# 320 products an edge, selectors with four parts, and window sums turned by VectorE on their way out of PSUM

## The chip, the core and the metric

The kernel runs on one core of one Trainium2 chip. A core has five engines with a queue of instructions each: TensorE (PE, with its weight loads as PEld), VectorE (DVE), ScalarE (ACT), GpSimd (POOL) and SyncE (SP, here only for DMA). The metric is the device time of one execution in microseconds (us). A time is the median of several runs.

## The reference

One layer of a graph network in float32, 12500 nodes and 400000 edges, the edges sorted by target node. A node has 160 numbers: 64 scalars (y0) and 32 vectors of three components (y1). Cut to what matters:

```python
h = relu(layernorm(x))                      # 12500 x 160
y0, y1 = h[:, :64] @ W_l1_0, einsum(h1, W_l1_1)
w = silu(edge_attr_16 @ fc_W1) @ fc_W2      # 192 weights an edge: w_a 64, w_b 64, w_c 32, w_d 32
ys0, ys1 = y0[src], y1[src]
e0, e1 = edge_attr_4[:, :1], edge_attr_4[:, 1:]
mid_a = w_a * ys0 * e0                      # 64
mid_d = w_d * einsum('euc,ec->eu', ys1, e1) # 32, over sqrt(3)
mid_b = (w_b * ys0)[:, :, None] * e1[:, None, :]   # 64 x 3
mid_c = (w_c * e0)[:, :, None] * ys1               # 32 x 3
z0 = scatter_add(concat(mid_a, mid_d), dst)        # 96 a node
z1 = scatter_add(concat(mid_b, mid_c), dst)        # 96 x 3 a node
out = x + skip(h) + linear(z0, z1)                 # W_l2_0, W_l2_1
```

(Scale factors and the factor of each node are left out.)

## The kernel before

**Node phase (0 to about 120 us).** Layer norm, the maps to y0 and y1, and y written to DRAM (y_d, 160 numbers a row). It also loads and scales the weights; wo holds the weights of the linear step behind the sums, as three blocks of 128 rows.

**Edge phase.** The edges stand as 3125 tiles of 128 edges, one edge a partition. A *batch* is GT = 4 tiles; there are 782. Sums are made over *windows* of 32 target nodes: 24 tiles a window where nodes have many edges, then 12, 8, 6, 4 and 3, in order of the edges, 598 windows in all; four windows make a *group* of 128 nodes (150 groups). The order of the code is the order of the work on every engine; nothing is rearranged. For batch b the loop issues:

1. weigh(b + 2): two matmuls on PE (L606) give the 192 edge weights of four tiles in a PSUM buffer pw (two buffers). ACT multiplies w_a and w_c by e0, tile by tile (L524, four instructions), and copies e1 and the window-relative target into the same buffer (L525).
2. In the first three batches of a group, a step for the group before: turn (three transposes on PE, L656, and ACT's copy za, L658), linear (three matmuls, L665, ACT's copy os, L667, and a 0/1 matrix "place" by DVE, L669), add (two matmuls, L677). Behind the products of the third, accumulate adds to the output rows (DVE, L688).
3. select(b + 1) and products(b + 1), all on DVE. The selector (L618, L620) is a 128 x 128 matrix a tile: for each of 32 nodes of the window the 0/1 entry, and that times each of the three parts of e1. The products (L530 to L537) are 256 an edge: mid_a, w_c e0 y1, mid_d (with a product, a sum over components and a product), and w_b y0.
4. sums(b): per tile one matmul (L640), selector by products, 128 x 256, added up in a PSUM buffer pz (two buffers). Rows 96 to 127 of the result are the plain sums, rows 0 to 95 those times e1; of the 128 x 256 only the plain sums of the first 192 columns and the e1 sums of the last 64 are used. When a window ends, ACT copies them out of PSUM in four instructions (L646, L648) into zs, 32 rows a window. A matmul is recorded as two in the profile.
5. gather(b + 4): four indirect DMAs on POOL (L573), each fetching 128 rows of y_d. The first of them waits, by an added dependency, for the last matmul of sums(b).
6. Every fourth batch, hidden_pair: two matmuls with 512 columns (L586) and ACT's silu (L591), for the hidden layer of the edge weights.

Between these steps stand smaller ones for the skip term (L705 to L731), and for 16 batches whose rows come from the core's own maps in place of y_d.

Engines wait for each other in these ways that the change touches: DVE's selector waits for ACT's L525 (of its batch); PE's sums wait for DVE's products; ACT's copies wait for PE's sums, and stand in ACT's queue ahead of the scaling for a later batch; PE's transposes wait for ACT's copies of the group's last window and stand ahead of the sums of the next batch; POOL waits for sums.

A path for edges whose target lies outside the window (a loop behind the main one) is compiled and does not run on this input.

Of the kernel before, what the change touches and what calls it, by code (L numbers as in the profile page):

```python
# [10 lines left out]
F32 = mybir.dt.float32  # L11
# [7 lines left out]
P = 128  # L19
# [6 lines left out]
PC = 256  # L26
ZC = 384
# [23 lines left out]
def kernel(  # L51
# [85 lines left out]
    wo = const.tile([P, 3, D], F32, name="wo")  # L137
# [11 lines left out]
    wor = ip.tile([P, 3, D], F32, name="wor")  # L149
# [115 lines left out]
    def edge_weight_loads():  # L265
# [14 lines left out]
        load(wor[0:M0 + M1, 0, 0:M0], w_l2_0)  # L280
        for rows, k, c in ((slice(96, P), 0, 0), (slice(0, 32), 1, 1), (slice(32, 64), 1, 2)):
            load(wor[rows, k, o1(c)], w_l2_1[M0:, :])
        for rows, k, c in ((slice(64, P), 1, 0), (slice(0, 64), 2, 1), (slice(64, P), 2, 2)):
            load(wor[rows, k, o1(c)], w_l2_1[0:M0, :])
# [5 lines left out]
    def edge_weights():  # L290
# [3 lines left out]
        nc.vector.tensor_scalar(wo[M0:M0 + M1, 0, 0:M0], wo[M0:M0 + M1, 0, 0:M0], 1.0 / math.sqrt(3.0), None, ALU.mult)  # L294
# [226 lines left out]
    def scale(pw, ev, n):  # L521

        for k in range(n):
            nc.scalar.activation(pw[:, k, 0:96], pw[:, k, 0:96], AF.Copy, scale=ev[:, k, 0:1])  # L524
        nc.scalar.activation(pw[:, :n, NW:NW + 4], ev[:, :n, 1:5], AF.Copy)  # L525

    def multiply(pr, tmp, wt, yg, n):

        y1 = yg[:, :n, M0:].rearrange("p t (c u) -> p t c u", c=3)
        nc.vector.tensor_tensor(tmp[:, :n, 0:3, :], y1, wt[:, :n, NW:NW + 3].unsqueeze(3).to_broadcast([P, n, 3, M1]),  # L530
                                ALU.mult)
        nc.vector.tensor_reduce(tmp[:, :n, 3, :], tmp[:, :n, 0:3, :].rearrange("p t c u -> p t u c"), AX.X, ALU.add)  # L532
        nc.vector.tensor_mul(pr[:, :n, 192:PC], wt[:, :n, 96:160], yg[:, :n, 0:M0])  # L533
        nc.vector.tensor_mul(pr[:, :n, 0:M0], wt[:, :n, 0:M0], yg[:, :n, 0:M0])  # L534
        nc.vector.tensor_mul(pr[:, :n, 96:192].rearrange("p t (c u) -> p t c u", c=3),  # L535
                             wt[:, :n, M0:96].unsqueeze(2).to_broadcast([P, n, 3, M1]), y1)
        nc.vector.tensor_mul(pr[:, :n, M0:96], wt[:, :n, 160:NW], tmp[:, :n, 3, :])  # L537

    with (
        tc.tile_pool(name="selp", bufs=4) as selp,  # L540
        tc.tile_pool(name="prod", bufs=3) as prod,
        tc.tile_pool(name="tmp", bufs=1) as tmpp,
# [8 lines left out]
        hids, rows, wts, sels, z_ps, z_sb, zT, o_sb, prs, sums_ps, summed = ({} for _ in range(11))  # L551
# [62 lines left out]
        def select(b):  # L614

            n, wt = slots_of(b), wts[b]
            sel = sels[b] = selp.tile([P, GT, 4, WN], F32, name="sel")[:, :n, :, :]
            nc.vector.tensor_tensor(sel[:, :, 3, :], iota[:, 0:WN].unsqueeze(1).to_broadcast([P, n, WN]),  # L618
                                    wt[:, :n, NW + 3:NW + 4].to_broadcast([P, n, WN]), ALU.is_equal)
            nc.vector.tensor_tensor(sel[:, :, 0:3, :], sel[:, :, 3:4, :].to_broadcast([P, n, 3, WN]),  # L620
                                    wt[:, :n, NW:NW + 3].unsqueeze(3).to_broadcast([P, n, 3, WN]), ALU.mult)

        def products(b):
            wt, yg = wts.pop(b), rows.pop(b)
            pr = prod.tile([P, GT, PC], F32, name="pr")
            tmp = tmpp.tile([P, GT, 4, M1], F32, name="tmp")
            multiply(pr, tmp, wt, yg, slots_of(b))
            prs[b] = pr

        def sums(b):  # L630
# [3 lines left out]
            for k, t in enumerate(tiles_of(b)):  # L634
# [7 lines left out]
                if last:  # L642
                    if w == 0:
                        z_sb[g] = post.tile([P, ZC], F32, name="zs")
# [169 lines left out]
        for b in range(NB):  # L814
# [13 lines left out]
            if g and k < K:  # L828
                (turn, linear, add)[k](g - 1)
# [202 lines left out]
```

## Time and profile before

| | |
|---|---|
| median of three runs | 4765.01 us (4756.0 to 4784.77) |
| profiled execution | 4774.96 us |
| its span, first to last instruction | 4773.1 us |
| granted TensorE clock, mean | 0.868 |
| PE busy | 78% of the span |
| DVE, POOL busy | 62% each |
| ACT busy | 46% |
| first and last gather start | 115.4 and 4749.3 us |

The span is what the profile covers; 1.9 us of the execution lie around it. Busy shares are averages over the whole span, and an engine that is not busy may be the one that everything waits for: POOL counts as busy only while it works on a gather (0.95 us of the 1.25 us from one to the next), so that a POOL with nothing but gathers would show about 76%. A releaser named "remote" means that the profile has no instruction of this core to put the end of the wait down to.

### The profile page before, as it was taken

What the parts mean: (1) busy time and instruction counts of PE and PEld (TensorE: products, weight loads), DVE (VectorE), ACT (ScalarE), POOL (GpSimd) and SP (SyncE); (2) the same over time, 40 slices, a digit from 0 to 9 for tenths busy, and PEclk for the clock granted to TensorE, in tenths of its full rate; (3) what the DMA queues carried; (4) which work ended last, traced back from release to release, by engine and by line L of the source; (5) the groups of instructions that cost most, each with busy time, mean ns of one, the idle gap of its engine ahead of it and who ended that gap; (6) DMA issues with size and microseconds to landing.
All of it is one profiled execution on the core that took longest, in us unless ns stands there. A gap on an engine that the chain in (4) does not pass through costs nothing.

```text
span 4773.1 us, 53679 instructions
## 1 busy us (share of the span) xinstructions
PE 3720.7 (78%) x13928; PEld 2551.0 (53%) x13928; DVE 2953.5 (62%) x8027; ACT 2205.2 (46%) x7512; POOL 2962.3 (62%) x3145
## 2 busy tenths in 40 slices
PE   7777778787777777777777777778777887788877
PEld 6455555455555554555555555555555555555555
DVE  5666666666666666656566656656566666666655
ACT  5333334344444443444444444444444455555555
POOL 5666666666656666666666666656665666665655
PEclk8888888888988888888888888888888888988988
DMA  7222222222222222222222222222222222222224
GB/s 192 67 60 64 63 62 65 60 65 66 61 62 65 66 70 66 66 63 69 65 69 63 66 62 64 67 62 64 62 66 65 64 66 63 68 66 66 64 58 115
DMA packets 262414, 328.99 MB, mean 69 GB/s; under 512 B 82776, under 2 KB 212104, under 8 KB 262104
## 3 DMA queue, kind: packets, MB, share of 16 engines
q0 software_dynamic: 150128, 256.23, 21.8%
q1 hardware_dynamic: 111478, 69.00, 5.2%
q8 instruction: 113, 1.85, 0.2%
q14 instruction: 197, 1.61, 0.1%
q10 hardware_dynamic: 498, 0.30, 0.0%
HBM read 307.66 MB, written 17.61 MB: 68 GB/s over the span
## 4 chain that ended last, share of the span: by engine, by line
PE 56%; another core or an unknown queue 15%; ACT 12%; issue 8%; DVE 7%; POOL 0%; DMA 0%; DVEq 0%; SPq 0%; ACTq 0%
PE pz L640 23%; PE pw L606 17%; ACT pw L524 6%; PE px L586 6%; PE px L665 3%; ACT zs L648 2%; PE px L656 2%; PE px L677 2%; DVE tmp L532 1%; DVE tmp L530 1%; ACT zs L646 1%; DVE pr L535 1%; DVE pr L534 1%; ACT pw L525 1%
## 5 line engine op out<-in xcount | busy, mean ns | idle before, releaser
L573 POOL DMA_INDIRECT yg<-y_d,src_q x3061 | 2896.2, 946 | 1748.8 <-issue 787.3
L640 PE MATMUL pz<-pr,sel 128*128 128x256 f32 x6250 | 1682.1, 417 | 38.1 <-ACT zs L648 36.1
L606 PE MATMUL pw<-w,hT 128*128 128x384 f32 x3126 | 1314.2, 547 | 304.3 <-DVE pr L537 111.7
L524 ACT ACTIVATE pw<-pw,ev 128x96 f32<-128x96 f32 x3125 | 984.9, 315 | 1199.1 <-remote 303.9
L640 PEld LDWEIGHTS pz<-pr,sel 128*128 128x128 f32 x6250 | 1289.4, 214 | 279.0 <-ACT zs L648 46.4
L606 PEld LDWEIGHTS pw<-w,hT 128*128 128x128 f32 x3126 | 619.2, 208 | 822.5 <-issue 377.2
L618 DVE TENSOR_TENSOR sel<-iota,pw 128x128 f32<-128x128 f32 x782 | 221.5, 283 | 1255.8 <-ACT pw L525 680.1
L646 ACT ACTIVATE zs<-pz 32x192 f32<-32x192 f32 x598 | 193.4, 323 | 801.0 <-remote 345.2
L532 DVE TENSOR_REDUCE tmp<-tmp 128x128 f32<-128x384 f32 x782 | 463.6, 593 | 31.1 <-remote 3.6
L586 PE MATMUL px<-xe,w 32*128 32x512 f32 x782 | 334.2, 750 | 161.0 <-ACT za L658 102.8
L620 DVE TENSOR_TENSOR sel<-sel,pw 128x384 f32<-128x384 f32 x782 | 432.7, 553 | 39.8 <-remote 8.0
L530 DVE TENSOR_TENSOR tmp<-yg,pw 128x384 f32<-128x384 f32 x766 | 419.6, 548 | 55.4 <-DMA yg<-y_d,src_q 48.8
L535 DVE TENSOR_TENSOR pr<-pw,yg 128x384 f32<-128x384 f32 x766 | 419.2, 547 | 0.0
L648 ACT ACTIVATE zs<-pz 32x64 f32<-32x64 f32 x1794 | 383.1, 214 | 24.4
L656 PE MATMUL px<-ident,zs 128*128 128x128 f32 (+1 forms) x450 | 129.3, 362 | 301.3 <-ACT zs L646 259.2
L533 DVE TENSOR_TENSOR pr<-pw,yg 128x256 f32<-128x256 f32 x766 | 317.0, 414 | 0.0
L534 DVE TENSOR_TENSOR pr<-pw,yg 128x256 f32<-128x256 f32 x766 | 316.9, 414 | 0.0
L591 ACT ACTIVATE hT<-px 128x512 f32<-128x512 f32 x391 | 216.1, 594 | 212.2 <-PE px L586 86.7
L656 PEld LDWEIGHTS px<-ident,zs 128*128 128x128 f32 (+1 forms) x450 | 69.7, 159 | 411.9 <-ACT zs L646 307.7
L586 PEld LDWEIGHTS px<-xe,w 32*128 32x128 f32 x782 | 90.2, 218 | 282.3 <-ACT za L658 123.4
L665 PEld LDWEIGHTS px<-wo,za 128*128 128x128 f32 x900 | 163.6, 222 | 108.0 <-ACT hT L591 36.2
L537 DVE TENSOR_TENSOR pr<-pw,tmp 128x128 f32<-128x128 f32 x782 | 219.2, 280 | 0.0
(139 smaller groups left out, 2210.2 us busy)
## 6 DMA issues: line engine op xcount, KB each, us to landing
yg<-y_d,src_q POOLq DMA_INDIRECT x3061
xe<-in_e SPq DMA_DIRECT2D x784, 32.0 KB
xs<-in_x SPq DMA_DIRECT2D x48, 160.0 KB
acc<-in_x SPq DMA_DIRECT2D x11, 640.0 KB
y_d<-ys SPq DMA_DIRECT2D x11, 640.0 KB
out<-acc SPq DMA_DIRECT2D x11, 640.0 KB
raw<-in_e SPq DMA_DIRECT2D x32, 192.0 KB
src_q<-in_src SPq DMA_DIRECT2D x32, 48.0 KB
```

The source lines that it names most:

```text
L524: nc.scalar.activation(pw[:, k, 0:96], pw[:, k, 0:96], AF.Copy, scale=ev[:, k, 0:1])
L530: nc.vector.tensor_tensor(tmp[:, :n, 0:3, :], y1, wt[:, :n, NW:NW + 3].unsqueeze(3).to_broadcast([P, n, 3, M1]), ALU.mult)
L532: nc.vector.tensor_reduce(tmp[:, :n, 3, :], tmp[:, :n, 0:3, :].rearrange("p t c u -> p t u c"), AX.X, ALU.add)
L533: nc.vector.tensor_mul(pr[:, :n, 192:PC], wt[:, :n, 96:160], yg[:, :n, 0:M0])
L534: nc.vector.tensor_mul(pr[:, :n, 0:M0], wt[:, :n, 0:M0], yg[:, :n, 0:M0])
L535: nc.vector.tensor_mul(pr[:, :n, 96:192].rearrange("p t (c u) -> p t c u", c=3), wt[:, :n, M0:96].unsqueeze(2).to_broadcast([P, n, 3, M1]) ...
L573: fetch = nc.gpsimd.indirect_dma_start(out=yg[:, slot(t), :], out_offset=None, in_=y_d, in_offset=bass.IndirectOffsetOnAxis(ap=ev4[t // BL ...
L586: nc.tensor.matmul(ph, w1[r, :], xe[r, :], start=True, stop=True)
L606: nc.tensor.matmul(pw[:, 2 * k:2 * k + m, 0:NW], hT[:, o:o + P], w2[:, :m, :], start=True, stop=True)
L620: nc.vector.tensor_tensor(sel[:, :, 0:3, :], sel[:, :, 3:4, :].to_broadcast([P, n, 3, WN]), wt[:, :n, NW:NW + 3].unsqueeze(3).to_broadcast ...
L640: mm = nc.tensor.matmul(pz[:, 0:PC], sel[:, slot(t), :, :], pr[:, slot(t), :], start=o == 0, stop=last)
L648: nc.scalar.activation(zs[:, 192 + M0 * c:192 + M0 * (c + 1)], pz[WN * c:WN * (c + 1), 192:PC], AF.Copy)
```

## The change

It moves the four parts of e (e0 and the three of e1) out of the products and into the selectors. The selector's 128 columns are now the 0/1 entry times each of e0, e1x, e1y and e1z. The products of an edge are then free of e, and 320 in number: w_a y0, w_c y1 (96), w_b y0 and w_d y1 (96). ACT no longer scales; one instruction copies e's four parts and the relative target. On DVE the reduction over components goes, two products are one instruction and the others two of the same shape.

A window's sums are 128 x 320. Of them the first 32 rows (times e0) of the first 160 columns are used, and all rows of the last 160. VectorE takes them out of PSUM as transposes in squares of 32 by 32 (L639, L640 of the changed kernel), so that za, the operand of the linear step, is there without a turn on PE. za has five blocks of 128 rows in place of three, and some of them are zero weights; linear has five matmuls. The turn step goes, and linear and add stay at the second and third batch of the next group.

```diff
-PC = 256
-ZC = 384
+PC = 320
+ZC = 448
+ZK = 5
...
     def scale(pw, ev, n):
-        for k in range(n):
-            nc.scalar.activation(pw[:, k, 0:96], pw[:, k, 0:96], AF.Copy, scale=ev[:, k, 0:1])
-        nc.scalar.activation(pw[:, :n, NW:NW + 4], ev[:, :n, 1:5], AF.Copy)
+        nc.scalar.activation(pw[:, :n, NW:NW + 5], ev[:, :n, :], AF.Copy)
-    def multiply(pr, tmp, wt, yg, n):
+    def multiply(pr, wt, yg, n):
         y1 = yg[:, :n, M0:].rearrange("p t (c u) -> p t c u", c=3)
-        nc.vector.tensor_tensor(tmp[:, :n, 0:3, :], y1, wt[:, :n, NW:NW + 3].unsqueeze(3).to_broadcast([P, n, 3, M1]),
-                                ALU.mult)
-        nc.vector.tensor_reduce(tmp[:, :n, 3, :], tmp[:, :n, 0:3, :].rearrange("p t c u -> p t u c"), AX.X, ALU.add)
-        nc.vector.tensor_mul(pr[:, :n, 192:PC], wt[:, :n, 96:160], yg[:, :n, 0:M0])
-        nc.vector.tensor_mul(pr[:, :n, 0:M0], wt[:, :n, 0:M0], yg[:, :n, 0:M0])
-        nc.vector.tensor_mul(pr[:, :n, 96:192].rearrange("p t (c u) -> p t c u", c=3),
-                             wt[:, :n, M0:96].unsqueeze(2).to_broadcast([P, n, 3, M1]), y1)
-        nc.vector.tensor_mul(pr[:, :n, M0:96], wt[:, :n, 160:NW], tmp[:, :n, 3, :])
+        nc.vector.tensor_mul(pr[:, :n, :].rearrange("p t (x u) -> p t x u", x=2)[:, :, :, 0:M0],
+                             wt[:, :n, 0:NW].rearrange("p t (x u) -> p t x u", x=2)[:, :, :, 0:M0],
+                             yg[:, :n, 0:M0].unsqueeze(2).to_broadcast([P, n, 2, M0]))
+        for x in range(2):
+            nc.vector.tensor_mul(pr[:, :n, D * x + M0:D * (x + 1)].rearrange("p t (c u) -> p t c u", c=3),
+                                 wt[:, :n, 96 * x + M0:96 * (x + 1)].unsqueeze(2).to_broadcast([P, n, 3, M1]), y1)
...
-        def select(b):
...
         def products(b):
+            n, wt, yg = slots_of(b), wts.pop(b), rows.pop(b)
+            own = selp.tile([P, GT, WN], F32, name="own")
             sel = sels[b] = selp.tile([P, GT, 4, WN], F32, name="sel")[:, :n, :, :]
+            pr = prs[b] = prod.tile([P, GT, PC], F32, name="pr")
+            nc.vector.tensor_tensor(own[:, :n, :], iota[:, 0:WN].unsqueeze(1).to_broadcast([P, n, WN]),
+                                    wt[:, :n, NW + 4:NW + 5].to_broadcast([P, n, WN]), ALU.is_equal)
+            nc.vector.tensor_tensor(sel, own[:, :n, :].unsqueeze(2).to_broadcast([P, n, 4, WN]),
+                                    wt[:, :n, NW:NW + 4].unsqueeze(3).to_broadcast([P, n, 4, WN]), ALU.mult)
+            multiply(pr, wt, yg, n)
...
-                    nc.scalar.activation(zs[:, 0:192], pz[96:P, 0:192], AF.Copy)
-                    for c in range(3):
-                        nc.scalar.activation(zs[:, 192 + M0 * c:192 + M0 * (c + 1)],
-                                             pz[WN * c:WN * (c + 1), 192:PC], AF.Copy)
-        def turn(g):
...
+                        zT[g] = post.tile([P, ZK, P], F32, name="za")
+                    pz, at_w = z_ps.pop((g, w)), slice(WN * w, WN * (w + 1))
+                    nc.vector.transpose(zT[g][:, :, at_w], pz[:, D:PC].rearrange("p (k u) -> p k u", k=ZK))
+                    nc.vector.transpose(zT[g][0:32, :, at_w], pz[0:32, 0:D].rearrange("p (k u) -> p k u", k=ZK))
         def linear(g):
-            for k in range(3):
-                nc.tensor.matmul(po[:m, :], za[:, k, :m], wo[:, k, :], start=k == 0, stop=k == 2)
+            for k in range(ZK):
+                nc.tensor.matmul(po[:m, :], za[:, k, :m], wo[:, k, :], start=k == 0, stop=k == ZK - 1)
...
-            if g and k < K:
-                (turn, linear, add)[k](g - 1)
+            if g and 0 < k < K:
+                (linear, add)[k - 1](g - 1)
...
-                select(b + 1)
                 products(b + 1)
```

The loads and the scaling of wo follow its five blocks (more and smaller loads on SP in the node phase).

How the order of instructions moves, at three places. Rows of consecutive instructions of one engine; names are buffers, and x2 is two alike. First DVE, around the step linear of a group in the middle of the edges. Before:

```order
L618 TENSOR_TENSOR sel<-iota,pw 128x4x32
L620 TENSOR_TENSOR sel<-sel,pw 128x4x96
L530 TENSOR_TENSOR tmp<-yg,pw 128x4x96
L532 TENSOR_REDUCE tmp<-tmp 128x4x32
L533 TENSOR_TENSOR pr<-pw,yg 128x4x64
L534 TENSOR_TENSOR pr<-pw,yg 128x4x64
L535 TENSOR_TENSOR pr<-pw,yg 128x4x96
L537 TENSOR_TENSOR pr<-pw,tmp 128x4x32
L669 TENSOR_SCALAR place<-iota,at 128x256
```

The same place on DVE in the changed kernel:

```order
L617 TENSOR_TENSOR own<-iota,pw 128x128
L619 TENSOR_TENSOR sel<-own,pw 128x512
L530 TENSOR_TENSOR pr<-pw,yg 128x8x64
L534 TENSOR_TENSOR pr<-pw,yg 128x4x96 x2
L650 TENSOR_SCALAR place<-iota,at 128x256
L617 TENSOR_TENSOR own<-iota,pw 128x128
L619 TENSOR_TENSOR sel<-own,pw 128x512
L530 TENSOR_TENSOR pr<-pw,yg 128x8x64
L534 TENSOR_TENSOR pr<-pw,yg 128x4x96 x2
L639 STREAM_TRANSPOSE za<-pz 128x5x32
L640 STREAM_TRANSPOSE za<-pz 32x5x32
```

Eight instructions a batch are five, and at the end of a window two transposes have come in, which wait for the last matmul of that window's sums: behind the products of the batch after it, ahead of those of the next.

Second, ACT at such a place, where a window ends in nearly every batch. Before:

```order
L525 ACTIVATE pw<-ev 128x4x4
L658 ACTIVATE za<-px 128x384
L646 ACTIVATE zs<-pz 32x192
L648 ACTIVATE zs<-pz 32x64 x3
L591 ACTIVATE hT<-px 128x512 x2
L524 ACTIVATE pw<-pw,ev 128x96 x4
L525 ACTIVATE pw<-ev 128x4x4
L667 ACTIVATE os<-px 128x160
L646 ACTIVATE zs<-pz 32x192
L648 ACTIVATE zs<-pz 32x64 x3
```

ACT there in the changed kernel:

```order
L696 ACTIVATE sT<-px 128x512
L525 ACTIVATE pw<-ev 128x4x5
L588 ACTIVATE hT<-px 128x512 x2
L525 ACTIVATE pw<-ev 128x4x5
L648 ACTIVATE os<-px 128x160
```

The scalings, the copies of window sums and the turn's copy are gone; no instruction of ACT waits for sums any more.

Third, PE from the last sums of a group to the linear step of it. Before:

```order
L640 MATMUL pz<-pr,sel 128x256 x4
L606 MATMUL pw<-w_94,hT 128x2x192 x2
L656 MATMUL px<-ident,zs 128x128 x3
L640 MATMUL pz<-pr,sel 128x256 x4
L586 MATMUL px<-xe,w_93 128x512 x2
L606 MATMUL pw<-w_94,hT 128x2x192 x2
L665 MATMUL px<-wo,za 128x160 x3
```

And in the changed kernel:

```order
L633 MATMUL pz<-pr,sel 128x320 x4
L603 MATMUL pw<-w_94,hT 128x2x192 x2
L633 MATMUL pz<-pr,sel 128x320 x4
L583 MATMUL px<-xe,w_93 128x512 x2
L603 MATMUL pw<-w_94,hT 128x2x192 x2
L646 MATMUL px<-wo,za 128x160 x5
```

The three transposes between weigh and the next batch's sums are gone, the sums have 320 columns, and the linear step, at its old place, has five matmuls.

86 lines of the change are left out of this document (39 added, 47 removed).

## The prediction

> **What bounds the kernel now.** I read the busy totals and the chain first, then single gathers in the timeline, then the stages, then the waits.
>
> ```profile
> PE 3720.7 (78%) x13928; PEld 2551.0 (53%) x13928; DVE 2953.5 (62%) x8027; ACT 2205.2 (46%) x7512; POOL 2962.3 (62%) x3145
> PE 56%; another core or an unknown queue 15%; ACT 12%; issue 8%; DVE 7%; POOL 0%; DMA 0%; DVEq 0%; SPq 0%; ACTq 0%
> PE pz L640 23%; PE pw L606 17%; ACT pw L524 6%; PE px L586 6%; PE px L665 3%; ACT zs L648 2%; PE px L656 2%; PE px L677 2%; DVE tmp L532 1%; DVE tmp L530 1%; ACT zs L646 1%; DVE pr L535 1%; DVE pr L534 1%; ACT pw L525 1%
> ```
>
> No engine is full. PE is nearest with 78% and carries 56% of the chain, but 15% of the chain (716 us of 4773) is waiting that the trace can put on no engine. The stages say more (the last row is all gathers: shortest, median and longest in ns, first and last start):
>
> ```profile
> 120.00:1000.00 880.00, 671.31 (x2449) 458.97 (x2448) 556.28 (x1445) 341.67 (x1122) 550.93 (x582) 0.87 0.25 63
> 1000.00:2000.00 1000.00, 771.89 (x2853) 526.11 (x2852) 631.36 (x1661) 425.44 (x1424) 632.38 (x669) 0.87 0.26 65
> 3000.00:4000.00 1000.00, 792.89 (x2880) 535.44 (x2881) 606.16 (x1627) 496.04 (x1725) 614.52 (x650) 0.85 0.26 64
> L573 POOL DMA_INDIRECT yg<-y_d,src_q x3061: 940/946/1337, 115.4 to 4749.3; - x192
> ```
>
> Columns: the stretch, its length, then busy time and count of PE, PEld, DVE, ACT, POOL, and the granted clock. ACT's work grows from 0.39 to 0.50 of a stage, because windows close more often late in the edges; the number of gathers per 1000 us stays at 661, 669 and 650. So the pace does not follow ACT's load, and hardly the windows. On average a gather comes every (4749.3 − 115.4)/3060 = 1.514 us, and the gathers fill the span from 115.4 on: whatever the change does, it does it by letting gathers go sooner or later.
>
> ```profile
> 2519.85 0.95 POOL L573 DMA_INDIRECT yg<-y_d,src_q  x1 [0.30 <-issue]
> 2522.77 0.94 POOL L573 DMA_INDIRECT yg<-y_d,src_q  x1 [1.97 <-PE px L677]
> 2524.01 0.94 POOL L573 DMA_INDIRECT yg<-y_d,src_q  x1 [0.30 <-issue]
> ...
> 2536.51 0.95 POOL L573 DMA_INDIRECT yg<-y_d,src_q  x1 [0.30 <-issue]
> 2540.18 0.94 POOL L573 DMA_INDIRECT yg<-y_d,src_q  x1 [2.72 <-remote]
> ```
>
> Inside a run gathers start 1.25 us apart; between runs POOL stands still until the sums it waits for are known. Twelve gathers took 2540.18 − 2522.77 = 17.41 us, 1.45 each. What ends such a stop is odd (start, length, engine, line; the idle time before and its releaser in brackets; sums count two records a tile):
>
> ```profile
> 2530.30 1.89 PE L640 MATMUL pz<-pr,sel 128*128 128x256 f32 x8
> 2539.95 0.32 ACT L646 ACTIVATE zs<-pz 32x192 f32<-32x192 f32 x1 [5.94 <-remote]
> 2541.62 1.97 PE L665 MATMUL px<-wo,za 128*128 128x160 f32 x6 [4.33 <-ACT hT L591]
> ...
> 4756.73 0.32 ACT L646 ACTIVATE zs<-pz 32x192 f32<-32x192 f32 x1 [0.45 <-PE pz L640]
> ```
>
> The sums end at 2532.19, but ACT's first copy of them starts at 2539.95, after the run of gathers has ended and 5.94 us idle, put down to "remote": no instruction of the trace. After the last gather (4749.3) such a copy follows its sums after less than half a microsecond. I read it so: **while POOL issues gathers, PE's completion signals can reach ACT and POOL late, mostly when the run ends.** A long run then costs one hold per 8 or 12 gathers, a short one a hold per 4. Taking 1.457 us (11.66 us for 8, which fits the twelve above) for runs of 8 and more, the edges would end at 115.4 + 3060 × 1.457 = 4574, and with the 23.8 us behind the last gather the span would be 4598. The profiled span is 4773.1, so **about 175 us is lost above that floor**. This loss is what a change of waits can win, and what it can make larger.
>
> **The change part by part.** The sums are against the profiled run, 4774.96 us, which lies 10 us above the median of 4765.01.
>
> ```profile
> L640 PE MATMUL pz<-pr,sel 128*128 128x256 f32 x6250 | 1682.1, 417 | 38.1 <-ACT zs L648 36.1
> L665 PE MATMUL px<-wo,za 128*128 128x160 f32 x900 | 172.5, 334 | 46.7 <-ACT hT L591 28.3 <-ACT za L658 15.3 <-DVE acc L731 1.7
> L656 PE MATMUL px<-ident,zs 128*128 128x128 f32 (+1 forms) x450 | 129.3, 362 | 301.3 <-ACT zs L646 259.2
> L524 ACT ACTIVATE pw<-pw,ev 128x96 f32<-128x96 f32 x3125 | 984.9, 315 | 1199.1 <-remote 303.9
> L646 ACT ACTIVATE zs<-pz 32x192 f32<-32x192 f32 x598 | 193.4, 323 | 801.0 <-remote 345.2
> L648 ACT ACTIVATE zs<-pz 32x64 f32<-32x64 f32 x1794 | 383.1, 214 | 24.4
> L658 ACT ACTIVATE za<-px 128x384 f32<-128x384 f32 x150 | 73.0, 487 | 82.0 <-remote 65.7 <-PE px L586 8.0 <-PE pz L640 3.3
> L618 DVE TENSOR_TENSOR sel<-iota,pw 128x128 f32<-128x128 f32 x782 | 221.5, 283 | 1255.8 <-ACT pw L525 680.1
> L620 DVE TENSOR_TENSOR sel<-sel,pw 128x384 f32<-128x384 f32 x782 | 432.7, 553 | 39.8 <-remote 8.0
> L532 DVE TENSOR_REDUCE tmp<-tmp 128x128 f32<-128x384 f32 x782 | 463.6, 593 | 31.1 <-remote 3.6
> L533 DVE TENSOR_TENSOR pr<-pw,yg 128x256 f32<-128x256 f32 x766 | 317.0, 414 | 0.0
> L534 DVE TENSOR_TENSOR pr<-pw,yg 128x256 f32<-128x256 f32 x766 | 316.9, 414 | 0.0
> L537 DVE TENSOR_TENSOR pr<-pw,tmp 128x128 f32<-128x128 f32 x782 | 219.2, 280 | 0.0
> L736 DVE TENSOR_TENSOR oh<-iota,xp 128x512 f32<-128x512 f32 x16 | 11.0, 689 | 0.0
> L688 DVE SCALAR_TENSOR_TENSOR acc<-px,a_sb,acc 128x160 f32 x300 | 114.6, 382 | 149.4 <-PE px L677 71.8 <-PE pz L640 28.0 <-remote 21.5
> ```
>
> *PE.* A tile's sums (two records) took 1682.1/3125 = 0.538 us for 256 columns; 320 columns add a quarter, 0.135 × 3125 = **+421**. The linear step took 172.5/450 = 0.383 a matmul; two more for each of 150 groups, **+115**. The turn goes: **−129**. Together +406, 0.52 us a batch of 782, and PE's busy time becomes about 4127, 88% of a span of 4690. These durations are at the mean clock, 0.87 in the stages' rows. In one stretch of the stop above it was half:
>
> ```profile
> 2539.00:2540.00 1.00, 0.00 (x0) 0.00 (x0) 0.00 (x0) 0.05 (x1) 0.00 (x0) 0.50 0.00 0
> ```
>
> PE (first column) had stood idle and the granted clock (0.50) with it. [...]
>
> *ACT.* The four scalings of a batch go (−985), the four copies at a window's end (−193 − 383) and the turn's copy (−73): −1634, so about 571 is left. No work is added but a fifth value in L525. ACT stops being anyone's limit: between weigh's matmuls and DVE stand 0.2 us instead of four scalings and a copy, some 1.4 us less.
>
> *DVE, batch work.* The 512-element instructions are put at 689 (L736). Selector: 689 in place of 553. Two products of 256 elements become one of 512: 689 in place of 414 + 414. The reduction and the last product go (593 + 280); the product with e1 becomes a second one of L535's shape, with no difference. Sum −876 ns × 782 = **−685**. If the broadcast reads of the new 512-element ones run slower, by no more than a second pass over 128 elements (283) each, that is 443 less of the gain.
>
> *DVE, transposes.* 598 windows × 2, a kind of instruction the trace does not show. From below L618's 283 ns (128 elements, half of its input from PSUM) = 338; from above L532's 593, the only one that reads in another order than it stores = 709. I take 0.32, between L618 and L688's 382 for 160 elements from PSUM and nearer the first, since one of the two has only a quarter of the lanes: **+383**. DVE in sum −302 (between −347 and +24 for the transposes alone). [...]
>
> *What moves.* The copies out of PSUM leave ACT's queue, where they stood ahead of a later batch's scaling, and enter DVE's, between products(b+1) and products(b+2). So the late signal that stopped ACT now stops DVE. Behind the waiting transpose stand the selectors and products of b+2, then PE's sums for b+2 and, through the PSUM buffer that DVE frees, weigh's matmuls for b+4; behind the sums POOL's next gathers. PE itself loses a wait: L656 stood 301.3 us idle, 259.2 of it for ACT's copies, with sums of the next batch behind. The linear step moves to where the data has long been ready.
>
> ```profile
> DVE sel L618 <- ACT pw L525: 680.1, 208, 9.7
> DVE sel L618 <- ACT pw L524: 415.9, 164, 8.4
> POOL yg L573 <- remote: 337.3, 141, 3.9
> ```
>
> DVE already stands 1096 us waiting for ACT (total, times, longest), mostly because ACT is itself held. That wait goes over into the transposes' wait for PE; it does not vanish. DVE's own work is no limit: 2953 − 302 = 2651, 57%.
>
> *Loads at the start.* wor is loaded in more pieces, on SP, before 115.4; PE's 89% of the first 120 us is the cover, and I cost it at nothing. If uncovered it is a few microseconds.
>
> **The sum.** By the chain's shares of 4773: sums 23% = 1098, a quarter more, +274; linear 3% = 143, two thirds more, +95; the copies L646 and L648 were on it for 3% = 143 of their 576 busy, a quarter, and the transposes with the same share give +96. Gone: L524 6%, L646, L648, L656 together 5%, L532 1%, 12% = 573. Net −108. By the gathers: the round trip from gather to sums gets shorter by about 1.0 us of products (593 + 280 and 414 + 414 − 689, less what the selector and the extra order hide) and longer by 0.54 of sums, about half a microsecond better, and the turn no longer cuts runs short, but the holds remain. So I let half of the 175 come back: −87, **4688, said as 4690 us**. Both reckonings agree on the sign and roughly on the size; the chain's assumes that nothing else takes the freed place, so I stay above it.
>
> **The rivals.**
>
> *Slower: DVE waits for held sums while PE is nearly full.* In the stage from 3000 on PE worked 792.89/650 × 8 = 9.76 us for 8 gathers; with 2 × 0.52 it is 10.8, in a run that lasts 11.66 at its best. If each run then has one hold that stops DVE, and with it PE, for the mean of POOL's "remote" waits, 337.3/141 = 2.39, eight gathers take 13.2 us instead of 8 × 1.514 = 12.11, +1.08. In the second half, some 1800 gathers or 225 runs of 8, three runs in five so hit give +146; the first half, where windows close in fewer batches, keeps 40% of the 87. Together +111, about **4890**; with every run +243 − 35, 4983. It decides where a stop of DVE is longer than PE's slack of 0.9 us a run. For it: PE on 56% of the chain, and its half clock after stops. Against: DVE now has 0.9 us a batch more slack, and ACT's queue can't hold anything.
>
> *No effect.* The gathers' own 1.25 us and the holds set the pace, whoever is held: 650 to 669 gathers per 1000 us at quite different loads of ACT speak for it, and the loss stays 175: **4775**, within 1% of before (1% is about what a measurement of this kernel can tell from no change). The case that the change fails to shift work is part of it: PE's extra 406 may just fill its gaps.
>
> *Much faster.* If the holds come from ACT's many instructions and not from POOL's gathers, they go with them, and POOL runs at its own 1.25: 115.4 + 3825 + 23.8 = 3964, which PE's 4127 forbids; at 1.35 it gives **4270**.
>
> **How the numbers follow.** Forecast (4600 to 4717) 0.42; slower 0.38; no effect 0.14; much faster 0.06. Faster by over 1% is the first and last, 0.48; the sign is so open because PE is charged 406 us in any case, and the gain lies in waits. The range leaves out the much faster case and the worst of the slower one: from 4540 (1.438 a gather, 1% better than the run of twelve had) to 4930 (midway between 4890 and 4983). The forecast's own range is 4600 to 4717.
>
> **What would show it.** In the profile after: PE busy 4050 to 4150; ACT near 570; DVE near 2650; two transposes of about 0.3 us; gathers in runs of 8 or more at 1.46 a gather, and fewer runs of 4. The forecast is wrong if DVE's waits for PE's sums exceed the 1096 us that it waited for ACT, if PE's clock falls below 0.86, or if the gathers of the late stages fall below 640 per 1000 us; the no-effect case shows as gathers per 1000 us unchanged and PE's idle time smaller by just what it is charged.

## The result, and the profile after

The changed kernel takes 4709.57 us (median of 4 runs, 4703.56 to 4713.89) against 4770.42 for the kernel before in the same comparison: a ratio of 0.9872, with a 95% interval of 0.9838 to 0.9905. That is 1.3% faster; 4690 was forecast, and the range was 4540 to 4930. The profiled execution has a span of 4708.8 us, 64.3 less than before.

The page of the changed kernel, first busy time, then the chain by engine and by line:

```profile
PE 3891.7 (83%) x14078; PEld 2542.2 (54%) x14078; DVE 2736.7 (58%) x6877; ACT 581.6 (12%) x1845; POOL 2968.3 (63%) x3145
PE 66%; another core or an unknown queue 15%; issue 7%; DVE 7%; ACT 2%; ACTq 1%; POOL 0%; DMA 0%; DVEq 0%; SPq 0%; POOLq 0%
PE pz L633 31%; PE pw L603 19%; PE px L646 6%; PE px L583 3%; DVE pr L534 2%; PE px L658 2%; DVE pr L530 1%; ACT hT L588 1%; ACTq L525 1%; DVE za L640 1%; DVE za L639 1%; PE po L457 1%; PE px L704 1%; POOL yg L570 0%
```

ACT has gone from 46% to 12%. PE is busier by 171 us and DVE less busy by 217. The share of the chain that waits for nothing the trace shows is 15% as before. The groups (busy us, mean ns of one, idle time before and what ended it):

```profile
L570 POOL DMA_INDIRECT yg<-y_d,src_q x3061 | 2901.9, 948 | 1681.5 <-issue 795.2
L633 PE MATMUL pz<-pr,sel 128*128 128x320 f32 x6250 | 1950.3, 457 | 17.6 <-DVE za L640 15.2
L603 PE MATMUL pw<-w,hT 128*128 128x384 f32 x3126 | 1233.8, 519 | 208.7 <-DVE pr L534 135.6
L639 DVE STREAM_TRANSPOSE za<-pz 128x160 f32<-128x160 f32 x598 | 206.5, 345 | 1298.9 <-PE pz L633 551.3
L534 DVE TENSOR_TENSOR pr<-pw,yg 128x384 f32<-128x384 f32 x1532 | 773.5, 546 | 0.0
L530 DVE TENSOR_TENSOR pr<-pw,yg 128x512 f32<-128x512 f32 x766 | 523.2, 683 | 126.8 <-DMA yg<-y_d,src_q 118.3
L646 PE MATMUL px<-wo,za 128*128 128x160 f32 x1500 | 320.2, 376 | 294.4 <-ACT hT L588 198.2
L619 DVE TENSOR_TENSOR sel<-own,pw 128x512 f32<-128x512 f32 x782 | 536.9, 687 | 28.1 <-issue 1.2
L617 DVE TENSOR_TENSOR own<-iota,pw 128x128 f32<-128x128 f32 x782 | 200.0, 256 | 177.1 <-ACT pw L525 133.8
L640 DVE STREAM_TRANSPOSE za<-pz 32x160 f32<-32x160 f32 x598 | 202.1, 338 | 20.5
L669 DVE SCALAR_TENSOR_TENSOR acc<-px,a_sb,acc 128x160 f32 x300 | 113.9, 380 | 113.2 <-PE px L658 70.8
```

The first row answers for the whole change. GpSimd's idle time ahead of gathers fell from 1748.8 to 1681.5, by 67.3 us, and the span by 64.3: what the change won shows as less time in which the gathers stand still. Counted from their starts (over 1.4 us apart is a stop), there are 351 stops in place of 388, and each is as long as before (2.10 and 2.08 us beyond the 1.25): fewer stops, not shorter ones. DVE's idle time has moved as well: 1255.8 us ahead of the selector became 1298.9 ahead of the transpose, and 177.1 ahead of the selector.

By stages (length, then busy time and count of PE, PEld, DVE, ACT, POOL, granted clock):

```profile
120.00:1000.00 880.00, 726.11 (x2542) 459.89 (x2541) 482.68 (x1086) 118.17 (x368) 572.80 (x604) 0.91 0.24 65
1000.00:2000.00 1000.00, 819.98 (x2904) 527.66 (x2903) 562.78 (x1337) 120.22 (x385) 639.00 (x674) 0.92 0.24 66
3000.00:4000.00 1000.00, 826.94 (x2970) 543.32 (x2971) 602.26 (x1520) 103.95 (x340) 624.20 (x659) 0.91 0.24 65
```

In the first 880 us 604 gathers start in place of 582, in the later ones 674 and 659 in place of 669 and 650 (and 672 in place of 663 from 2000 to 3000, not shown). So half of the gain, 22 of the 45 gathers by which it is ahead at 4000 us, falls in the stage where windows are long and close seldom. The clock is 0.91 to 0.92 in place of 0.85 to 0.87.

The holds are still there. The timeline of the changed kernel at a window's end (rows of PE, POOL, ACT and DVE, others left out):

```profile
2119.97 1.01 DVE L534 TENSOR_TENSOR pr<-pw,yg 128x384 f32<-128x384 f32 x2
...
2124.24 2.32 PE L633 MATMUL pz<-pr,sel 128*128 128x320 f32 x8
...
2132.18 0.94 POOL L570 DMA_INDIRECT yg<-y_d,src_q  x1 [0.31 <-issue]
2135.28 0.30 ACT L648 ACTIVATE os<-px 128x160 f32<-128x160 f32 x1 [4.03 <-remote]
2135.34 0.35 DVE L639 STREAM_TRANSPOSE za<-pz 128x160 f32<-128x160 f32 x1 [9.73 <-remote]
2135.64 0.95 POOL L570 DMA_INDIRECT yg<-y_d,src_q  x1 [2.52 <-remote]
```

The batch's sums end at 2126.56, and those of the window that L639 reads at 2125.48, inside the same row. ACT, DVE and POOL, which wait for different results of PE, go on within 0.36 us of each other, 8.7 us after the batch's sums, when the run of gathers has ended. Taking for each of the 598 windows the time from the end of its own last matmul to the start of the first instruction that reads its sums (ACT's L646 before, DVE's L639 after), 162 windows were read over 4 us late before, and 121 after.

### The profile page after: what moved, and what is told of

Read it like the earlier page. It is cut to its first block, busy times and chain, and to the rows that moved or that the text cites. A ratio compares the mean times of both kernels' runs of the same rounds, so it can differ in the third digit from the quotient of the medians.

```text
span 4708.8 us, 46910 instructions
## 1 busy us (share of the span) xinstructions
PE 3891.7 (83%) x14078; PEld 2542.2 (54%) x14078; DVE 2736.7 (58%) x6877; ACT 581.6 (12%) x1845; POOL 2968.3 (63%) x3145
## 4 chain that ended last, share of the span: by engine, by line
PE 66%; another core or an unknown queue 15%; issue 7%; DVE 7%; ACT 2%; ACTq 1%; POOL 0%; DMA 0%; DVEq 0%; SPq 0%; POOLq 0%
PE pz L633 31%; PE pw L603 19%; PE px L646 6%; PE px L583 3%; DVE pr L534 2%; PE px L658 2%; DVE pr L530 1%; ACT hT L588 1%; ACTq L525 1%; DVE za L640 1%; DVE za L639 1%; PE po L457 1%; PE px L704 1%; POOL yg L570 0%
## 5 line engine op out<-in xcount | busy, mean ns | idle before, releaser
L570 POOL DMA_INDIRECT yg<-y_d,src_q x3061 | 2901.9, 948 | 1681.5 <-issue 795.2
L633 PE MATMUL pz<-pr,sel 128*128 128x320 f32 x6250 | 1950.3, 457 | 17.6 <-DVE za L640 15.2
L603 PE MATMUL pw<-w,hT 128*128 128x384 f32 x3126 | 1233.8, 519 | 208.7 <-DVE pr L534 135.6
L639 DVE STREAM_TRANSPOSE za<-pz 128x160 f32<-128x160 f32 x598 | 206.5, 345 | 1298.9 <-PE pz L633 551.3
L534 DVE TENSOR_TENSOR pr<-pw,yg 128x384 f32<-128x384 f32 x1532 | 773.5, 546 | 0.0
L530 DVE TENSOR_TENSOR pr<-pw,yg 128x512 f32<-128x512 f32 x766 | 523.2, 683 | 126.8 <-DMA yg<-y_d,src_q 118.3
L646 PE MATMUL px<-wo,za 128*128 128x160 f32 x1500 | 320.2, 376 | 294.4 <-ACT hT L588 198.2
L619 DVE TENSOR_TENSOR sel<-own,pw 128x512 f32<-128x512 f32 x782 | 536.9, 687 | 28.1 <-issue 1.2
L646 PEld LDWEIGHTS px<-wo,za 128*128 128x128 f32 x1500 | 290.2, 246 | 364.7 <-ACT hT L588 226.5
L525 ACT ACTIVATE pw<-ev 128x20 f32<-128x20 f32 x782 | 149.6, 191 | 2624.1 <-PE pw L603 970.4
L617 DVE TENSOR_TENSOR own<-iota,pw 128x128 f32<-128x128 f32 x782 | 200.0, 256 | 177.1 <-ACT pw L525 133.8
L640 DVE STREAM_TRANSPOSE za<-pz 32x160 f32<-32x160 f32 x598 | 202.1, 338 | 20.5
L669 DVE SCALAR_TENSOR_TENSOR acc<-px,a_sb,acc 128x160 f32 x300 | 113.9, 380 | 113.2 <-PE px L658 70.8
```

What stands on the lines that cost most here:

```text
L530: nc.vector.tensor_mul(pr[:, :n, :].rearrange("p t (x u) -> p t x u", x=2)[:, :, :, 0:M0], wt[:, :n, 0:NW].rearrange("p t (x u) -> p t x u ...
L534: nc.vector.tensor_mul(pr[:, :n, D * x + M0:D * (x + 1)].rearrange("p t (c u) -> p t c u", c=3), wt[:, :n, 96 * x + M0:96 * (x + 1)].unsqu ...
L570: fetch = nc.gpsimd.indirect_dma_start(out=yg[:, slot(t), :], out_offset=None, in_=y_d, in_offset=bass.IndirectOffsetOnAxis(ap=ev4[t // BL ...
L603: nc.tensor.matmul(pw[:, 2 * k:2 * k + m, 0:NW], hT[:, o:o + P], w2[:, :m, :], start=True, stop=True)
L619: nc.vector.tensor_tensor(sel, own[:, :n, :].unsqueeze(2).to_broadcast([P, n, 4, WN]), wt[:, :n, NW:NW + 4].unsqueeze(3).to_broadcast([P, ...
L633: mm = nc.tensor.matmul(pz[:, 0:PC], sel[:, slot(t), :, :], pr[:, slot(t), :], start=o == 0, stop=last)
```

## The experiments

The theory at this point: **H**, GpSimd's gathers set the pace, because PE's signals reach others late while they are issued; the change wins where it makes fewer things wait for such a signal. Against it: **E**, the engines' own loop sets the time (PE is 66% of the chain), and GpSimd follows.

Ratios below are to the kernel before, measured beside each; the changed kernel stands at 0.9872.

### Without gathers

```diff
-            for k, t in enumerate(tiles_of(b)):
-                fetch = nc.gpsimd.indirect_dma_start(
-                    out=yg[:, slot(t), :], out_offset=None, in_=y_d, in_offset=...)
-                if k == 0 and b - AHEAD in summed:
+            n, lo = slots_of(b), b % 24 * GT * P
+            fetch = nc.sync.dma_start(yg[:, :n, :], y_d[lo:lo + n * P, :].rearrange("(t p) u -> p t u", p=P))
+            if True:
+                if b - AHEAD in summed:
                     tc.add_manual_dep(fetch.ins, summed[b - AHEAD], ...)
```

The kernel before with this edit:

> The kernel before with its rows of y fetched by one plain load a batch from SyncE (the same 640 byte rows in number, from fixed places) in place of four indirect gathers on GpSimd; what is computed from them is therefore not the layer. Theory H (GpSimd's gathers and the completion signals that come late while they run set the time): without gathers no wait of several us ends at 'remote', PE idles little, its clock rises to 0.97 or more, and the time falls to what PE needs, 3720 x 0.87 = 3240 at full clock plus the two ends, 3350 to 3700 us. Theory E (the engines' own loop sets the time and GpSimd only follows): within 3% of 4770.

The changed kernel with it:

> The changed kernel with the same replacement of its gathers. Theory H: 3892 x 0.906 = 3526 of PE at full clock plus the ends, 3600 to 3900 us, and now slower than the kernel before with the same replacement, by about PE's added work at full clock, 200 to 350 us. Theory E: within 3% of 4710, and still faster than before.

Measured: 3298.41 us (ratio 0.6887, 0.6847 to 0.6927) and 3541.87 (0.7395, 0.7353 to 0.7438). **Without gathers the change makes the kernel 7.4% slower** (3541.87/3298.41), and PE is busy for 96% and 98% of the time. Both times lie below H's ranges, by 52 and 58 us; their difference of 243 is inside the 200 to 350. The page, first of the kernel before, then of the changed one:

```profile
PE 3165.6 (96%) x13928; PEld 2305.5 (70%) x13928; DVE 2915.4 (89%) x8027; ACT 2203.7 (67%) x7512; POOL 65.8 (2%) x84
PE 78%; DVE 15%; ACT 4%; issue 2%; DMA 0%; SPq 0%; DVEq 0%; ACTq 0%
```

```profile
PE 3475.3 (98%) x14078; PEld 2317.9 (66%) x14078; DVE 2712.3 (77%) x6877; ACT 592.2 (17%) x1845; POOL 66.4 (2%) x84
PE 90%; DVE 7%; issue 0%; ACT 0%; DVEq 0%; ACTq 0%
```

"Another core or an unknown queue" has left the chain, and of the 598 windows none is read over 4 us late in either. The clock is 0.990 and 0.996. Near full clock the sums tell their price in full:

```profile
L640 PE MATMUL pz<-pr,sel 128*128 128x256 f32 x6250 | 1485.4, 381 | 0.0
```

```profile
L633 PE MATMUL pz<-pr,sel 128*128 128x320 f32 x6250 | 1817.9, 434 | 0.6 <-DVE za L640 0.6
```

That is +332.5 us, more than the difference of 243 between the two times. E is out: with gathers neither kernel runs at its own loop's speed.

Whose signals are late can be read directly. The trace also holds moments at which an engine raised its completion signal (not all: with gathers about six in ten of DVE's and ACT's, eight in ten of PE's). In the changed kernel 2367 of DVE's 2380 and 1034 of ACT's 1036 come within 0.1 us of the end of an instruction that raises one; of PE's only 1022 of 2231 do, and 136 come over 4 us behind the nearest such end. Without gathers 2727 of PE's 2796 come within 0.1 us. In the timeline above, PE's four instructions that raise it and end between 2124.40 and 2127.85 are matched by four raises between 2135.26 and 2135.44, and DVE's transpose starts at 2135.34. So PE's signals are held back, and the engines that wait for them are not slow themselves: DVE is busy for 2736.7 us with gathers and for 2712.3 without.

### Gathers that nothing reads

The plain loads as above, and behind them the four gathers of the batch, with the same dependency, into a tile "un" (three buffers) that no instruction reads.

> The changed kernel with plain loads for the rows that are used, and beside them the same gathers on GpSimd, paced by the same sums, into buffers that nothing reads. Theory H, by the issuing itself: the signals come as late as ever, since GpSimd issues as many gathers; 4600 to 4800 us. If instead the products' wait for the gathered rows (their landing) sets the time: near the run without gathers, under 4000 us.

Measured: 4738.10 us, ratio 0.9893 (0.9836 to 0.995), the time of the changed kernel. The long waits of DVE and ACT by "remote" are back (total, times, longest; first this run, then the changed kernel):

```profile
DVE za L649 <- remote: 478.4, 95, 13.7
ACT hT L598 <- remote: 422.4, 90, 12.8
```

```profile
DVE za L639 <- remote: 435.7, 86, 9.7
ACT hT L588 <- remote: 648.9, 112, 12.7
```

So it is not the rows' arrival that the time hangs on. That GpSimd issues 3061 gathers, with nobody reading what they fetch, costs 1196 us (4738.10 − 3541.87). Two things are in this sum. At 1.25 us each, with the 117.4 us ahead of the first and the 22.3 behind the last, the gathers alone need 3965 us, some 425 more than the kernel without them. The other 771 of the profiled span of 4735.8 are time in which they stop, waiting for sums.

### PE's larger sums taken back

```diff
-                mm = nc.tensor.matmul(pz[:, 0:PC], sel[:, slot(t), :, :], pr[:, slot(t), :], ...)
+                mm = nc.tensor.matmul(pz[:, 0:256], sel[:, slot(t), :, :], pr[:, slot(t), 0:256], ...)
-                    nc.vector.transpose(zT[g][:, :, at_w], pz[:, D:PC]...)
+                    nc.vector.transpose(zT[g][:, :, at_w], pz[:, 96:256]...)
```

> The changed kernel with the sums' matmuls over 256 of the 320 product columns (64 columns left out, so the sums are not complete); all else, the transposes too, stays. It takes back PE's largest added term, 1950 x 0.2 = 390 us of busy time. If PE is what the time is made of (66% of the chain): -150 us or more, below 4560. Theory H: PE fills its idle time, and the time moves by less than 60 us, 4650 to 4710.

Measured: 4715.0 us, 5 above H's range; ratio 0.985 (0.9805 to 0.9894), not to be told from the changed kernel's 0.9872. The sums' group, and then the page, show where the 330 us go:

```profile
L633 PE MATMUL pz<-pr,sel 128*128 128x256 f32 x6250 | 1620.1, 405 | 28.9 <-DVE za L640 19.1 <-issue 6.8 <-DVE za L639 1.6
```

```profile
PE 3642.9 (78%) x14078; PEld 2577.7 (55%) x14078; DVE 2728.5 (58%) x6877; ACT 581.6 (12%) x1845; POOL 2962.4 (63%) x3145
L570 POOL DMA_INDIRECT yg<-y_d,src_q x3061 | 2896.2, 946 | 1672.8 <-issue 803.2
```

PE is 249 us less busy, its granted clock in this run is 0.885 in place of 0.906, and GpSimd's idle time is 8.7 us less. The 64 added columns are free here, though the chain gives the sums 31% of the time.

### Parts taken out one by one

The kernel before without ACT's scaling (the four L524 a batch are left out):

```diff
-        for k in range(n):
-            nc.scalar.activation(pw[:, k, 0:96], pw[:, k, 0:96], AF.Copy, scale=ev[:, k, 0:1])
```

> The kernel before without ACT's four scalings by e0 a batch (985 us of ACT; the factor e0 is left out). Theory W (the gain is what the shorter way from weigh to DVE wins, by letting GpSimd's next run start earlier): 4680 to 4740 us. Rival T (the gain comes from the turn that is gone from PE): no change, 4750 to 4790.

Measured: 4718.63 us, ratio 0.9876 (0.9845 to 0.9907), −51 us.

The kernel before without the turn:

```diff
-            for k in range(3):
-                nc.tensor.transpose(pt[:, k, :m], zs[:m, P * k:P * (k + 1)], ident[:m, :m])
-            za = post.tile([P, 3, P], F32, name="za")
-            nc.scalar.activation(za[:, :, :m], pt[:, :, :m], AF.Copy)
-            zT[g] = za
+            zT[g] = za_all
```

> The kernel before without the turn: the three transposes a group and ACT's copy of them are left out and the linear step reads a constant; ACT's copies out of PSUM stay. Theory W: 4730 to 4780, at most 1% better, since 22 of the waits on PE go that held sums. Rival T: 4660 to 4720.

Measured: 4687.85 us, ratio 0.9825 (0.9801 to 0.985), −82 us. Each theory was right on one part and wrong on the other: W on the scaling, T on the turn. Both parts count. 129 us of PE and 73 us of ACT bring 82 us, and 985 us of ACT bring 51.

The changed kernel without the transposes (za is a constant), and with each transpose made twice:

```diff
-                    nc.vector.transpose(zT[g][:, :, at_w], pz[:, D:PC]...)
-                    nc.vector.transpose(zT[g][0:32, :, at_w], pz[0:32, 0:D]...)
```

> The changed kernel without the transposes: the linear step reads a constant, and DVE waits no more for sums. 409 us of DVE's work and its wait of 1300 us for sums go. If the new wait of DVE costs what the slower rival feared: 4620 or less, 2% under 4710. If the holds pass to whoever waits next: 4680 to 4720.

> The changed kernel with each transpose made twice (409 us more on DVE, nothing left out). If DVE's work lies on the path in each window: +200 us or more, 4900. If it fills idle time behind the holds: under 1% more, 4700 to 4755.

Measured: without them 4642.25 us, ratio 0.9731 (0.9708 to 0.9753), so the transposes with their wait cost 1.4%, some 67 us, a result between the two forecasts. With twice as many the kernel is not slower but faster: 4675.21, ratio 0.9799 (0.9775 to 0.9824), 0.7% under the changed kernel.

```profile
PE 3873.5 (83%) x14078; PEld 2495.4 (53%) x14078; DVE 3127.9 (67%) x8073; ACT 583.1 (12%) x1845; POOL 2976.9 (64%) x3145
L570 POOL DMA_INDIRECT yg<-y_d,src_q x3061 | 2910.5, 951 | 1633.8 <-issue 790.5
```

DVE does 391 us more and GpSimd stands 47.7 us less. DVE's added work has no price here. That what counts is how long a wait is, and where in GpSimd's pattern it falls, is my reading; the run does not show why it is a gain, which I had not expected.

### VectorE's turn undone alone

New products, selectors and sums as in the change; the sums leave PSUM by ACT, and PE turns them.

```diff
-                    nc.vector.transpose(zT[g][:, :, at_w], pz[:, D:PC]...)
-                    nc.vector.transpose(zT[g][0:32, :, at_w], pz[0:32, 0:D]...)
+                    for c in range(4):
+                        at0 = D if c else 0
+                        nc.scalar.activation(zs[:, :, WN * c:WN * (c + 1)], pz[WN * c:WN * (c + 1), at0:at0 + D]...)
...
+        def turn(g):
+            for lo, n in ((0, 3), (3, 2)):
+                pt = p_x.tile([P, 3, P], F32, name="px")
+                for k in range(n):
+                    nc.tensor.transpose(pt[:, k, :m], zs[:m, lo + k, :], ident[:m, :m])
+                nc.scalar.activation(za[:, lo:lo + n, :m], pt[:, :n, :m], AF.Copy)
```

> The changed products, selectors and 320-column sums, but the window sums leave PSUM by four copies of 32 x 160 on ACT and are turned on PE (five transposes a group in two buffers, two ACT copies), at the place of the old turn. Nothing is left out. Theory P (the gain is the turn that is gone from PE, as the kernel before without it gained 82 us): the gain is lost, 4740 to 4800. Rival S (the gain is ACT's scaling, which is gone here too, and ACT now does the copies with little else in its queue): 4690 to 4730.

Measured: 4856.61 us, ratio 1.0177 (1.0122 to 1.0231): slower than the kernel before, and by 3.1% slower than the change. Theory P holds, beyond its range. The groups of that run:

```profile
L570 POOL DMA_INDIRECT yg<-y_d,src_q x3061 | 2903.9, 949 | 1814.7 <-issue 788.8
L641 ACT ACTIVATE zs<-pz 32x160 f32<-32x160 f32 x2392 | 705.7, 295 | 1134.9 <-PE pz L633 463.6
L651 ACT ACTIVATE za<-px 128x384 f32<-128x384 f32 (+1 forms) x300 | 123.4, 435 | 384.0 <-remote 188.5
```

ACT is busy for 1410.2 us, far below what it did before. What is late is what passes from PE to ACT and back: 188.5 us of the wait for the turn's transposes end by "remote". I read it so: with the turn on PE a group's sums are handed from PE to ACT three times before the step add (window sums, turned block, linear's output), and each of these signals can come late; with VectorE's turn there are two, to DVE and to ACT. The e in the selectors alone, with such a turn, is a loss. This turn is larger than that of before (five transposes, two copies), so its 147 us are not the price of the old one.

### GpSimd's runs, longer and shorter

Without the dependency of the gathers on sums:

> The changed kernel without the added dependency of the gathers on the sums; GpSimd then waits only for a free buffer of rows (six, freed by DVE's products). Nothing is left out. Theory H: runs of gathers grow longer, and each holds the signals for longer; PE, ACT and DVE wait longer at a time, and the stops grow with the runs, so the gain per gather is small: 4650 to 4800, stops of 5 us and more. If the stops cost by their number: a third fewer of them, under 4550.

With a dependency for each gather, on the matmul of its own tile four batches ago:

> The changed kernel with each of a batch's four gathers waiting for the matmul of its own tile four batches ago, in place of the first gather for the last matmul. Nothing is left out. If signals come late because gathers are going on, shorter runs set them free sooner but stop GpSimd more often: runs of 1 to 4, 4700 to 4950. If the stops' number does not matter: within 1% of 4710.

Measured: 5180.44 us, ratio 1.0843 (1.0798 to 1.0888) without it; 4689.47, ratio 0.981 (0.9754 to 0.9866) with four. The waits of the run without it:

```profile
DVE za L635 <- remote: 797.0, 103, 14.1
POOL yg L570 <- DVE pr L534: 763.4, 153, 13.2
ACT pw L525 <- remote: 755.8, 109, 27.1
```

Counted from its gathers (starts over 1.4 us apart end a run), GpSimd stops 300 times in place of 351, and for 4.06 us more than the 1.25 at a time in place of 2.10. So fewer stops and longer runs are no gain as such: the waits by "remote" are longer (27.1 us at the longest), 364 of PE's 2071 recorded signals come over 4 us late in place of 136 of 2231, and GpSimd itself then waits for DVE's products. My expectation of 4650 to 4800, a small gain at best, was wrong in its direction: longer runs and longer waits came as I had said, but they cost 10% against the change. With four dependencies GpSimd stops 448 times, for 1.60 us each, and idles 22 us less than in the changed kernel; the interval of the ratio overlaps with the changed kernel's. The time is within the 1% of 4710 that I had given if the number of stops does not matter, but the runs did not all become short: 81 of 8 and 95 of 12 remain.

### The transposes a place later

```diff
         def products(b):
...
             nc.vector.tensor_tensor(sel, own[:, :n, :].unsqueeze(2)...)
+            turn_windows()        # the transposes of batch b - 2
             multiply(pr, wt, yg, n)
```

> The changed kernel with a batch's transposes moved in DVE's queue behind the two selector instructions of the batch after next (and still ahead of its products). Nothing is left out. If what DVE's wait for sums costs (68 us by the run without transposes) is the work standing behind it: 1 us of selector work is then done ahead of each wait, 4640 to 4690. If only the pattern of GpSimd's stops matters: anywhere within 1% of 4710.

Measured: 4682.44 us, ratio 0.982 (0.9778 to 0.9862). It lies in the bands of both forecasts, its interval overlaps with the changed kernel's, and doubled transposes gave as much, so that the reason (selector work ahead of the wait) is not shown.

Of all kernels that do the whole computation, the one with doubled transposes is the fastest, with an interval clear of the changed kernel's; as a design the one with later transposes is the sounder, by the medians 0.5% better than the change.

GpSimd's idle time and the span move together in all these runs. Since the gathers fill the span and take 0.95 us each in every run, they have to: the table says where the time shows, and not what causes it.

| kernel | GpSimd idle before gathers, us | span of the profiled run, us |
|---|---|---|
| before | 1748.8 | 4773.1 |
| changed | 1681.5 | 4708.8 |
| VectorE's turn undone | 1814.7 | 4847.2 |
| no dependency on sums | 2159.8 | 5197.6 |
| sums over 256 | 1672.8 | 4694.7 |
| before, no scaling | 1712.8 | 4733.1 |
| before, no turn | 1658.1 | 4687.4 |
| no transposes | 1601.7 | 4628.2 |
| transposes twice | 1633.8 | 4673.8 |
| transposes later | 1647.6 | 4679.1 |
| a dependency a gather | 1659.1 | 4681.7 |

## Why the prediction was right, and where it was not

**What bounds the kernel.** Right, and now shown: no gathers, no late signals (3298 and 3542 us), and gathers that nothing reads bring them back (4738). The prediction read it from single rows; the chain, which gave PE 56%, would have misled.

**The size.** The forecast let half of the 175 us above the floor of 4598 come back; 64 of 175 did (4773.1 to 4708.8). Direction and mechanism held. The size is in part luck: the fraction had been chosen, and it was 0.37 in place of 0.5. The floor rested on one run of 8 and one of 12, at 1.457 a gather; over all runs of 8 and more the kernel before took 1.473, which would put it at 4647, and the changed kernel takes 1.445. One detail of it failed: "the turn no longer cuts runs short" was to show in fewer runs of 4. Counted from the gathers there are 117 of them in place of 100; runs of 8 fell from 180 to 79, and runs of 12 and 16 rose from 91 to 144. So runs of 8 grew longer, and the 37 stops that are gone went there.

**PE, +406.** Measured +171 of busy time, so that the mark of 4050 to 4150 was missed. The sums brought +268 in place of +421, for two reasons: the columns' price is 22% for a quarter more (1485.4 to 1817.9 where the clock is 0.99), and PE's clock rose from 0.868 to 0.906, and with it L606 fell from 1314.2 to 1233.8 (1175.8 at 0.990, without gathers). Multiplied by the granted clock, PE's time went from 3720.7 × 0.868 = 3230 to 3891.7 × 0.906 = 3526, +296, where +406 at 0.868 comes to 352; this is an estimate, from L640's 1682.1 us at 0.868 and 1485.4 at 0.990, which are 1460 and 1471 by it. The granted clock was 0.868 with PE busy for 78% of the span and 0.906 with 83%, 0.990 and 0.996 without gathers (96% and 98%), but 0.885 with sums over 256 (78%): what sets it is not shown. The linear step brought +148 in place of +115. The loads at the start were covered, as the prediction had it (the first gather starts at 115.6 in place of 115.4 us), though PE's cover there was 89 us of the first 120, which is 74% and not 89%.

**ACT, 571 left.** 581.6. **DVE.** In time of instructions: a batch's are now 256 + 687 + 683 + 2 × 546 = 2718 ns in place of 3632, −715 us where −685 was worked out, and the transposes +409 (345 and 338 ns) where +383 was; −306 for −302. The busy time fell by 217 only, since neighbours overlap (two L534 of 0.546 take 1.01 us in the timeline's first row): overlaps hid 412 us of DVE's instructions before and 319 after. A transpose of 160 elements on each of 128 partitions took 0.345 us, under the 0.380 of L669 with as many from PSUM; on 32 partitions it took 0.338, so a quarter of the lanes saved next to nothing here, though the 0.32 had been chosen with a saving in mind.

**What moves.** Right in kind: DVE's wait for ACT became one for PE's sums. By its two main releasers, 551.3 and 435.7, it is 987 us, under the 1096 that the prediction had set as the mark of being wrong. But that mark too was the sum of two releasers; all idle time ahead of the transpose is 1298.9, against 1255.8 ahead of the selector before. So the wait moved and did not shrink, and whether the mark was passed depends on the count. PE's clock and the gathers of the late stages are on the good side of their marks.

**The reckoning by the chain's shares, −108.** It came near the result, by terms that were wrong one by one: sums +274 (taking them back moved nothing), scaling −286 (−51 when left out), copies and turn −239 (the turn alone −82; the copies were not tried alone), transposes +96 (67 with their wait). The four measured ones give −51 − 82 + 67 + 0 = −66, against −61 measured for the change. That is no proof: a larger turn cost 147, and the copies, the linear step and DVE's lighter products were not tried alone.

**The rivals.** The slower one rested on PE being nearly full, 10.8 us of an 11.66 us run. With sums over 256 columns nothing was won, so PE had room: it was busy for 83%, and its added 406 had come out as 171. (The 1800 gathers that the rival puts into the second half are those after 2000 us; the second half of the span has 1549, by which its 4890 would be some 20 us less.) Its other half, DVE's wait, is real and costs 1.4%. PE's added work does decide the sign once GpSimd is quiet: 7.4% slower. "Much faster" held that ACT's instructions make the holds; ACT now has a quarter of them, and 121 windows of 598 are still read late.

## What to carry to other kernels

When stops on several engines end at the same moment, by a releaser that the trace can't name, look for what ends just then (here a run of indirect gathers, behind which ACT, DVE and POOL went on within 0.36 us of each other), and price an edit by how many hand-overs between engines have to pass such a moment before busy time or shares of the chain; here the turn, 202 us of PE's and ACT's work, counted for more than 985 us of scaling. Take the suspect out and issue it for nobody: two runs settled here what no reading of the chain could. And a change that is a gain beside one bottleneck (fewer hand-overs for more PE work) turns into a loss of 7% when that bottleneck is gone, so it has to be measured again then.

## What the runs showed that I had not expected

- Indirect gathers that nothing reads cost 1196 us in a kernel that takes 3542 without them, though GpSimd shares no data with the engines that slow down. It is PE's signals that are kept back (in the changed kernel 136 of 2231 come over 4 us late), and not DVE's or ACT's (2367 of 2380 and 1034 of 1036 come within 0.1 us). By what part of the chip is open; nor do the runs part GpSimd's issuing from the gathers' own transfers.
- Doing the transposes twice (391 us more on DVE) made the kernel 0.7% faster. So a difference of 1% in such a kernel need not follow the work; I read it as the way that waits fall between runs of gathers, which no run shows.
- With gathers free to run ahead the kernel is 8.4% slower than before: pacing them by the sums is worth some 10% to the changed kernel (1.0843/0.9872).
